# Expert stage of a four-layer network: 25 tiles of 256 slots and 21 of 128 in place of 39 tiles of 256

## The chip, the cores and the metric

The kernel runs on one core of a Trainium2 chip, as one program. The metric is the device time of one execution in microseconds (us). The core has five engines that run side by side: PE (TensorE, matrix products and transposes, results in PSUM), DVE (VectorE), ACT (ScalarE), POOL (GpSimd, here mostly the issuer of indirect DMAs) and SP (SyncE, which issues plain DMAs). Each engine works through its own instructions in order and waits on semaphores for the others. Loading a stationary operand into PE is shown as a row of its own, PEld.

## The reference

Four layers work on x, four images of 256 channels and 32 x 32 points, that is 4096 tokens of 256 values. Layer 0 is a state-space layer, layer 1 a non-local gate. Layer 2 is attention and then a mixture of experts; layer 3 is a form of attention without a score matrix and then an LSTM over 1024 steps. The change lies in the mixture of experts:

```python
# layer 2 (the lines that matter; t is (4, 1024, 256))
t = t + _L2_attn_ref(_ln_t(t), ...)
t = t + _L2_ffn_ref(_ln_t(t), Wg, bg, W1, b1, W2, b2)   # TOP_K = 2, E = 8, H = 1024
```

In `_L2_ffn_ref` a gate (Wg, bg) picks the two best of eight experts for each token and weighs them with a softmax over the two. Expert e computes gelu(u W1[e] + b1[e]) W2[e] + b2[e], with W1[e] 256 x 1024 and W2[e] 1024 x 256. A token's result is the weighted sum of its two experts. That makes 8192 pairs of token and expert, split over the experts as the gate decides: the counts are known only at run time. Everything is f32.

## The kernel before

Layer 2 is `_layer2`: `_layer2_attention` goes over the four images, and `_layer2_experts` then runs the experts. `_head` prepares one image for the experts: it normalises the tokens, computes the gate, gives each pair a slot in a DRAM array `sorted` (one region of 4096 rows for each expert) and scatters the normalised rows, with their weight and their place in the result, to these slots by indirect DMAs from POOL (16 for an image, L1005). The head of image b runs beside the attention of image b + 1. Heads are generators; `beside(n)` and `next(parts, None)` take a few of their instructions between others. The head of the last image runs beside the first expert tiles.

A tile is 256 slots of one expert (TS = 256), two blocks of 128 (A = 2). Since counts are unknown when the program is built, the number of tiles is the one that always suffices: NTILE = 2 * 4096 / 256 + 7 = 39. Each expert's last tile may be partly empty; its empty slots are sent to rows of `results` that nothing reads. NFULL = 16 tiles are certain to be full from the first three images alone: `_first_tiles` finds their experts and slots, so that they can start before the last image's head is done. `_other_tiles` finds those of the other 23. `_table`, `_pick` and `_weight_rows` are their helpers: small DVE operations on tables of tiles by experts.

`_layer2_experts` then does for each tile j:

1. `gathered(j)`: POOL fetches the expert's weights, one row of 4360 floats for each of 128 partitions (2.23 MB, L1193), into one of three buffers (`moe_w1` holds one, `moe_w` two, chosen by j % 3), and the 256 rows, one indirect DMA for each block of 128 (L1198), into one of three `row` buffers. DVE copies the rows' places to `place` (L1207, L1209; three buffers). PE transposes the rows (four transposes to `pt`, L1213) and DVE copies them to `uT` (L1215).
2. The first product (L1230): for each of eight blocks of 128 hidden units, W1 is stationary and uT's 256 slots are moving, twice (256 inputs = 2 x 128). ACT applies gelu with the bias (L1234) and writes `hT`. The hidden units lie on the partitions, as the second product wants them.
3. The second product (L1244): for each block of 128 slots, eight products with hT stationary and W2 (256 columns) moving. DVE adds the bias (L1251) and multiplies by the weight (L1252); POOL scatters the 128 rows to `results` (L1253).

In the source `gathered(j + 1)` stands in the middle of the second product of tile j. Tile pools and a scheduler settle the order of each engine's instructions: an instruction can be moved ahead of others that don't bind it. In the built program POOL's order is: the scatter of tile t's first block, the weights of tile t + 3 (their buffer is that of tile t; they wait for its last reader, the bias addition L1251), the scatter of the second block, the rows of tile t + 3. `place` of a tile stands on DVE just ahead of the `uT` of the tile before it. The indirect DMAs take eight semaphores in turn, so that each also waits for the eighth before it.

During eight tiles SP loads one eighth of the tokens back into `x` for layer 3 (`x<-tokens`, 512 KB each, L1261). Layer 3 begins when the last scatter has landed.

Of the kernel before, what the change touches and what calls it, by code (L numbers as in the profile page):

```python
# [44 lines left out]
NTILE = 2 * T // TS + E - 1  # L45
# [3 lines left out]
NFULL = (2 * (T - L) - E * (TS - 1)) // TS  # L49
# [30 lines left out]
def _setup(s):  # L80
# [55 lines left out]
    s.results = nc.dram_tensor("results", (2 * T + NTILE * TS, D), F32, kind="Internal").ap()  # L136
# [579 lines left out]
def _layer2(s):  # L716
# [4 lines left out]
    with ExitStack() as ctx:  # L721
# [6 lines left out]
            row=ctx.enter_context(tc.tile_pool(name="moe_row", bufs=3)),  # L728
            scatters=[], full=[],
# [21 lines left out]
        first = _layer2_attention(s, m)  # L751
        _layer2_experts(s, m, first)


def _layer2_attention(s, m):
    nc, tc = s.nc, s.tc
    scale = D**-0.5
    with ExitStack() as ctx:
# [14 lines left out]
        first = None  # L773
        for b in range(B):
# [80 lines left out]
            if b == B - 1:  # L855

                first = _first_tiles(s, m)
    return first
# [225 lines left out]
def _first_tiles(s, m):  # L1084
# [3 lines left out]
    over = m.one.tile([P, E, NCH], F32, name="f_over")  # L1088
    edges = m.one.tile([P, NCH], F32, name="f_edges")
    nc.vector.tensor_scalar(edges, m.marks[:, :NCH], float(TS), float(TS), ALU.mult, ALU.add)  # L1090
    nc.vector.tensor_tensor(over, _bc(m.counts, 2, NCH), _bc(edges, 1, E), ALU.is_ge)
    full = m.one.tile([P, E], F32, name="f_full")
    nc.vector.tensor_reduce(full, over, AX.X, ALU.add)
    expert, mine, first = _table(s, m, "f", NFULL, full)
    rows = _weight_rows(s, m, "f", expert)

    base = m.one.tile([P, E], F32, name="f_base")
    nc.vector.tensor_scalar(base, first, -float(TS), 1.0, ALU.mult, ALU.add)
    nc.vector.tensor_add(base, base, m.first)
    at = _pick(s, m, "f", mine, base)  # L1100
    nc.vector.scalar_tensor_tensor(
        at, m.marks[:, :NFULL], float(TS), at, ALU.mult, ALU.add
    )
    slots = m.keep.tile([P, NFULL, 2], U32, name="f_slots")
    nc.vector.tensor_tensor(slots, _bc(at, 2, 2), _bc(s.token[:, :2], 1, NFULL), ALU.add)

    taken = m.keep.tile([P, E], F32, name="f_taken")
    nc.vector.tensor_scalar(taken, first, -1.0, float(NFULL), ALU.mult, ALU.add)
    nc.vector.scalar_tensor_tensor(taken, taken, 0.0, full, ALU.max, ALU.min)
    return rows, slots, taken  # L1110


def _other_tiles(s, m, taken):
# [3 lines left out]
    n = NTILE - NFULL  # L1117
    over = m.one.tile([P, E, NCH], F32, name="o_over")
    edges = m.one.tile([P, NCH], F32, name="o_edges")
    nc.vector.tensor_scalar_mul(edges, m.marks[:, :NCH], float(TS))  # L1120
    nc.vector.tensor_tensor(over, _bc(m.counts, 2, NCH), _bc(edges, 1, E), ALU.is_gt)
    tiles = m.one.tile([P, E], F32, name="o_tiles")
    nc.vector.tensor_reduce(tiles, over, AX.X, ALU.add)
    nc.vector.tensor_sub(tiles, tiles, taken)
    yield
    expert, mine, first = _table(s, m, "o", n, tiles)
    rows = _weight_rows(s, m, "o", expert)
    yield

    base = m.one.tile([P, E], F32, name="o_base")  # L1130
    nc.vector.tensor_sub(base, taken, first)
    own = _pick(s, m, "o", mine, base)
    nc.vector.tensor_add(own, own, m.marks[:, :n])
    yield
    at = m.one.tile([P, n, 2], F32, name="o_at")
    nc.vector.scalar_tensor_tensor(
        at, _bc(own, 2, 2), float(TS), _bc(s.token[:, :2], 1, n), ALU.mult, ALU.add
    )
    held = _pick(s, m, "o_held", mine, m.counts)
    yield  # L1140
    valid = m.one.tile([P, n, 2], F32, name="o_valid")
    nc.vector.tensor_tensor(valid, at, _bc(held, 2, 2), ALU.is_lt)

    nc.vector.tensor_scalar_add(expert, expert, -float(E))
    nc.vector.scalar_tensor_tensor(
        at, _bc(expert, 2, 2), float(T), at, ALU.mult, ALU.add
    )
# [5 lines left out]
    slots = m.keep.tile([P, n, 2], U32, name="o_slots")  # L1153
    nc.vector.tensor_copy(slots, at)
    yield
    added = m.keep.tile([P, n, 2], F32, name="o_added")
    nc.vector.tensor_scalar(valid, valid, -1.0, 1.0, ALU.mult, ALU.add)
    ahead = m.one.tile([P, n, 2], F32, name="o_ahead")
    nc.gpsimd.iota(
# [8 lines left out]
def _layer2_experts(s, m, first):  # L1168
# [3 lines left out]
    with ExitStack() as body:  # L1172
# [15 lines left out]
        def gathered(j):  # L1188
# [8 lines left out]
            for a in range(A):  # L1197
# [4 lines left out]
                if j < NFULL:  # L1202

                    m.full.append(got)
# [675 lines left out]
```

## Time and profile before

| what | us |
|---|---|
| median of 3 runs (3463.36 to 3467.37) | 3466.0 |
| the profiled execution, its own time | 3467.84 |
| span of the profile | 3465.9 |
| first weight fetch to the end of the last expert tile | 764 to 1362 |
| one expert tile, undisturbed | 14.26 |
| PE busy over the span | 3237.8 (93%) |
| DVE, ACT, POOL busy over the span | 1998.7, 1253.7, 399.1 |

The page's row of 40 slices shows where the stage lies (each slice is 86.6 us; slices 9 to 16 are the experts):

```profile
PE   7788899989999997899999999999999999999888
PEld 4465354447888886578888888888888888888776
DVE  5696434452211112747777777777777777776666
ACT  4633222223222221433433434334343343433333
POOL 0182002222533331000000000000000000000000
```

A busy PE means that a product was under way, and the ends of products are modelled, so the time of a tile is read from the starts of its instructions in the timeline. A line of the timeline has start and length in us, engine, source line, operation, what it writes and reads, shapes and count, and in square brackets the idle time before it and what ended it. In the groups the last column is the idle time of the engine just before them.

### The profile page before, as it was taken

To read this page: it belongs to the slowest core of one execution; us is meant where nothing else is said; L and a number is where in the kernel's file an instruction comes from. 1 tells how busy PE (TensorE), PEld (TensorE's weight loads), DVE (VectorE), ACT (ScalarE), POOL (GpSimd) and SP (SyncE) were. 2 spreads that over 40 slices of the span, in tenths; PEclk is the share of its full clock that TensorE was granted. 3 is DMA by queue.
4 is the path that set the end of the run, shared out by engine and by line. 5 is a ranking of instruction groups with operands and counts; after the bars stand their busy time and mean duration, and the time that the engine had idled before them with its cause. 6 is when DMAs were issued, how large, how long until landed. Compare 5 with 4: busy or idle time off the path is not lost.

```text
span 3465.9 us, 147036 instructions
## 1 busy us (share of the span) xinstructions
PE 3237.8 (93%) x65492; PEld 2546.7 (73%) x65492; DVE 1998.7 (58%) x8361; ACT 1253.7 (36%) x5081; POOL 399.1 (12%) x490
## 2 busy tenths in 40 slices
PE   7788899989999997899999999999999999999888
PEld 4465354447888886578888888888888888888776
DVE  5696434452211112747777777777777777776666
ACT  4633222223222221433433434334343343433333
POOL 0182002222533331000000000000000000000000
PEclk9899899999999998899999999999999999999999
DMA  1290001124556554100000000000000000000000
GB/s 68 78 298 25 0 0 37 37 100 165 198 197 224 209 193 162 49 2 5 4 11 4 4 11 4 5 10 4 11 4 5 10 4 5 10 5 4 10 4 10
DMA packets 79355, 189.58 MB, mean 55 GB/s; under 512 B 6592, under 2 KB 64256, under 8 KB 73728
## 3 DMA queue, kind: packets, MB, share of 16 engines
q0 software_dynamic: 16176, 116.06, 9.1%
q1 hardware_dynamic: 60624, 59.12, 5.8%
q8 instruction: 512, 8.39, 1.0%
q10 hardware_dynamic: 1920, 5.00, 0.4%
q14 instruction: 123, 1.01, 0.1%
HBM read 119.14 MB, written 61.02 MB: 52 GB/s over the span
## 4 chain that ended last, share of the span: by engine, by line
PE 46%; DVE 9%; ACT 4%; issue 2%; DMA 0%; ACTq 0%; SPq 0%; DVEq 0%
PE p_c L1721 11%; PE p_c L1712 8%; DVE turned L1762 6%; PE p_i L1712 5%; PE p_i L1721 5%; PE p_o L1721 5%; PE p_o L1712 5%; PE beside L1662 4%; ACT a_o L1763 2%; DVE x L1775 2%; ACT th L1773 1%; PE beside L1569 1%; PE p_u L1441 1%; PE p_mm L1412 1%; PE beside L1602 1%
## 5 line engine op out<-in xcount | busy, mean ns | idle before, releaser
L1763 ACT ACTIVATE add<-turned 128x8 f32<-128x8 f32 x1024 | 214.3, 209 | 1011.3 <-DVE turned L1762 1011.3
L1721 PE MATMUL p_c<-w_v,x 128*4 128x64 f32 x16368 | 416.6, 219 | 61.6 <-DVE x L1775 58.4
L1712 PE MATMUL p_c<-xg,shift 128*128 128x64 f32 x2048 | 446.0, 299 | 0.0
L1721 PE MATMUL p_i<-w_v,x 128*4 128x64 f32 x16368 | 417.4, 219 | 0.0
L1721 PE MATMUL p_o<-w_v,x 128*4 128x64 f32 x16368 | 417.3, 219 | 0.0
L1712 PE MATMUL p_i<-xg,shift 128*128 128x64 f32 x2048 | 407.0, 280 | 0.0
L1762 DVE STREAM_TRANSPOSE turned<-p_c 128x64 f32<-128x64 f32 x1024 | 255.9, 250 | 252.7 <-PE p_c L1721 219.4
L1712 PE MATMUL p_o<-xg,shift 128*128 128x64 f32 x2048 | 396.4, 275 | 0.0
L1712 PEld LDWEIGHTS p_c<-xg,shift 128*128 128x128 f32 x2048 | 304.9, 188 | 117.6 <-DVE turned L1762 0.4
L1721 PEld LDWEIGHTS p_c<-w_v,x 128*4 128x4 f32 x16368 | 228.0, 85 | 183.8 <-DVE x L1775 102.9
L1775 DVE TENSOR_TENSOR x<-a_o,th 128x8 f32<-128x8 f32 x1024 | 171.8, 168 | 246.6 <-ACT th L1773 246.6
L1712 PEld LDWEIGHTS p_o<-xg,shift 128*128 128x128 f32 x2048 | 311.4, 192 | 0.0
L1712 PEld LDWEIGHTS p_i<-xg,shift 128*128 128x128 f32 x2048 | 305.1, 188 | 0.0
L1230 PE MATMUL ph<-uT,w 128*128 128x256 f32 x1248 | 284.9, 386 | 19.0 <-DVE uT L1215 19.0
L1234 ACT ACTIVATE hT<-ph,w 128x256 f32<-128x256 f32 x312 | 147.9, 474 | 391.7 <-PE ph L1230 391.6
L1721 PEld LDWEIGHTS p_i<-w_v,x 128*4 128x4 f32 x16368 | 281.8, 87 | 0.5
L1244 PE MATMUL po<-w,hT 128*128 128x256 f32 x1248 | 282.0, 379 | 0.0
L1721 PEld LDWEIGHTS p_o<-w_v,x 128*4 128x4 f32 x16368 | 281.9, 87 | 0.0
L1230 PEld LDWEIGHTS ph<-uT,w 128*128 128x128 f32 x1248 | 240.4, 194 | 56.0 <-DVE uT L1215 22.2
L1762 DVE STREAM_TRANSPOSE turned<-p_i 128x64 f32<-128x64 f32 x1024 | 271.6, 265 | 1.1 <-PE p_i L1721 0.5
L1244 PEld LDWEIGHTS po<-w,hT 128*128 128x128 f32 x1248 | 234.1, 190 | 30.2
L1762 DVE STREAM_TRANSPOSE turned<-p_o 128x64 f32<-128x64 f32 x1024 | 255.9, 250 | 0.4 <-PE p_o L1721 0.3
(447 smaller groups left out, 4400.2 us busy)
## 6 DMA issues: line engine op xcount, KB each, us to landing
sorted<-zeros SPq DMA_DIRECT2D x32, 1032.0 KB, 15.0
y_in<-results SPq DMA_DIRECT2D x16, 512.0 KB, 6.0
x<-in_x_dram SPq DMA_DIRECT2D x8, 512.0 KB, 8.7
tokens<-rows SPq DMA_DIRECT2D x4, 1024.0 KB, 4.4
x<-tokens SPq DMA_DIRECT2D x8, 512.0 KB, 4.2
out_dram<-x_l SPq DMA_DIRECT2D x64, 64.0 KB, 1.7
results<-y,place POOLq DMA_INDIRECT x78, 4.3
w_l<-in_w_l_dram ACTq DMA_DIRECT2D x1, 1092.0 KB, 11.4
```

What stands on the lines that cost most here:

```text
L1230: nc.tensor.matmul(ph, w1[:, k, bass.ts(n, P)], uT[:, k, :], start=k == 0, stop=k == C - 1,)
L1234: nc.scalar.activation(hT[:, n, :], ph, AF.Gelu, bias=b1[:, n : n + 1])
L1244: nc.tensor.matmul(po, hT[:, n, bass.ts(a, P)], w2[:, n, :], start=n == 0, stop=n == NHC - 1,)
L1412: nc.tensor.matmul(p, wk[:, k, bass.ts(m, P)], u[:, k, b * L + i * W : b * L + (i + 1) * W], start=k == 0, stop=k == C - 1,)
L1441: nc.tensor.matmul(pu[c], rows[:, n, bass.ts(c, P)], kt, start=n == 0, stop=n == TPI - 1,)
L1569: nc.tensor.matmul(p, lhs[:, k, b, bass.ts(m, P)], rhs, start=k == 0, stop=k == C - 1)
L1662: nc.tensor.matmul(p[bass.ts(i, R), :], rows[:, k, bass.ts(g, R)], w_u[:, k, at : at + GQ // GC], start=k == 0, stop=k == C - 1, tile_posi ...
L1712: nc.tensor.matmul(p[:, :H], shift[:, row * B : row * B + P], xg[n][:, g, bass.ts(i, H)], start=True, stop=t == 0,)
L1721: nc.tensor.matmul(p[R * i : R * i + B, :H], hs[:, t - 1, bass.ts(k, B)], w_v[:, k, i * GQ + g * H : i * GQ + (g + 1) * H], start=False, s ...
L1762: nc.vector.transpose(zt.rearrange("p c w -> p (c w)"), pz[g][:, :H])
L1763: nc.scalar.activation(dst.rearrange("p (c b) -> p c b", c=C), zt[:, :, :B], f)
L1775: nc.vector.tensor_mul(h, a_o, th)
```

## The change

The 39 tiles become NTILE = 46: 17 full tiles from the first three images ("first"; rounded up where it was rounded down), 8 more full tiles that are certain once all four images are counted ("more"), and 21 half tiles of 128 slots for the rest. The order is the 17 first, then each of the 8 with two or three halves behind it (2, 3, 2, 3, 3, 2, 3, 3).

`_first_tiles` becomes the generator `_full_tiles`, called twice, and `_other_tiles` becomes `_half_tiles`, with the same small operations on one block for each tile. `gathered` is split: `fetched(j)` issues the DMAs and is called two tiles ahead, `turned(j)` copies the places and transposes the rows, and is called one tile ahead, ahead of the second block's product in a full tile and after the first four transposes in a half. The `row` pool has four buffers in place of three. The tokens are loaded back after each full tile of the second kind.

A half tile's first product is turned: uT's 128 slots are stationary and W1 is moving, 512 columns at a time (two PSUM banks, twice each). The result has the slots on the partitions; DVE copies it to SBUF (`raw`), PE transposes it in eight blocks of 128, and ACT applies gelu to each block of 128 columns. The second product is as before, once.

```diff
-NTILE = 2 * T // TS + E - 1
...
-NFULL = (2 * (T - L) - E * (TS - 1)) // TS
+NFULL = -(-(2 * (T - L) - E * (TS - 1)) // TS)
+NMORE = -(-(2 * T - E * (TS - 1)) // TS) - NFULL
+NHALF = (2 * T + E * (P - 1)) // P - 2 * (NFULL + NMORE)
+NTILE = NFULL + NMORE + NHALF
...
-            row=ctx.enter_context(tc.tile_pool(name="moe_row", bufs=3)),
+            row=ctx.enter_context(tc.tile_pool(name="moe_row", bufs=4)),
...
+    order = [("first", i) for i in range(NFULL)]
+    for i in range(NMORE):
+        order.append(("more", i))
+        order += [("half", h) for h in range(i * NHALF // NMORE, (i + 1) * NHALF // NMORE)]
...
         def last_image():
             yield from _head(s, m, B - 1, psum)
-            yield from _other_tiles(s, m, taken)
-
-        def gathered(j):
...
+            yield from _full_tiles(s, m, "more", NMORE, m.tiles["first"][2])
+            yield from _half_tiles(s, m, m.tiles["more"][2])
+
+        parts = last_image()
+
+        def fetched(j):
+
+            kind, i = order[j]
+            if kind != "first":
+                for _ in parts:
+                    pass
+            rows, slots = m.tiles[kind][:2]
             w = (wp if j % 3 else m.w).tile([P, NEXP], F32, name="w")
             nc.gpsimd.indirect_dma_start(
                 w, None, s.d["w12"], bass.IndirectOffsetOnAxis(rows[:, i : i + 1], 0)
             )
-            row = m.row.tile([P, A, ROW], F32, name="row")
+            A = slots.shape[2]
+            row = m.row.tile([P, 2, ROW], F32, name="row")
             for a in range(A):
...
+            return w, row[:, :A]
+
+        def turned(j):
...
+            place = rp.tile([P, 2], U32, name="place")[:, :A]
+            if kind == "half":
+                nc.vector.tensor_add(place, row[:, :, D + 1], m.tiles[kind][2][:, i, :])
+            else:
                 nc.vector.tensor_copy(place, row[:, :, D + 1])
...
+        held = {j: fetched(j) for j in range(2)}
+        ahead = turned(0)
+        for j, (_, tile) in enumerate(order):
+            if j + 2 < NTILE:
+                held[j + 2] = fetched(j + 2)
...
+            else:
+
+                raw = rp.tile([P, HID], F32, name="raw", bufs=2)
+                for i in range(HID // W):
+                    ph = ps.tile([P, W], F32, name="ph")
+                    for k in range(C):
+                        nc.tensor.matmul(
+                            ph, uT[:, k, :], w1[:, k, bass.ts(i, W)],
+                            start=k == 0, stop=k == C - 1,
+                        )
+                    nc.vector.tensor_copy(raw[:, bass.ts(i, W)], ph)
+                for i in range(HID // W):
+                    ph = ps.tile([P, W], F32, name="ph")
+                    for n in range(TPB):
+                        nc.tensor.transpose(
+                            ph[:, bass.ts(n, P)], raw[:, bass.ts(i * TPB + n, P)], s.ident
+                        )
+                    for n in range(TPB):
+                        gelu(i * TPB + n, ph[:, bass.ts(n, P)])
+                    if i == 0 and j + 1 < NTILE:
+                        ahead = turned(j + 1)
             for a in range(A):
+                if a == A - 1 == 1 and j + 1 < NTILE:
+                    ahead = turned(j + 1)
                 po = ps2.tile([P, D], F32, name="po")
...
-                if a == 0 and j + 1 < NTILE:
-                    ahead = gathered(j + 1)
...
-            if NFULL <= j < NFULL + NBLK:
-
-                i = j - NFULL
+            if j >= NFULL and A == 2:
+
                 got = nc.sync.dma_start(
-                    s.xr[:, bass.ts(i, TPB), :],
-                    s.tokens[bass.ts(i, W), :].rearrange("(n p) c -> p n c", p=P),
+                    s.xr[:, bass.ts(tile, TPB), :],
+                    s.tokens[bass.ts(tile, W), :].rearrange("(n p) c -> p n c", p=P),
                 )
```

Built, the changed program has POOL in the same order as before for weights (tile t + 3 behind tile t's last bias addition, the second scatter behind it). The rows of a tile now stand one tile earlier. `place` stands two tiles ahead of its use: of tile t + 3 behind the second scaling of tile t where t is full, of tile t + 2 ahead of the `raw` copies of tile t + 1 where tiles t and t + 1 are halves. It still has three buffers, so it waits for the scatter that last read its buffer: the one of tile t in the first case, of tile t - 1 in the second. The first tile's instructions up to its `uT`, and all of layer 3, stand in the same order.

## The prediction

> **What bounds the kernel now.** I read the page's parts 1, 2 and 5, then busy time by stretch of time, then the timeline of one tile of the expert stage, then its waits. All edits lie in that stage, from 764 us (first weight fetch) to 1362 us; the recurrence behind it (over 2000 us) is the same program before and after.
>
> ```profile
> L1230 PE MATMUL ph<-uT,w 128*128 128x256 f32 x1248 | 284.9, 386 | 19.0 <-DVE uT L1215 19.0
> L1234 ACT ACTIVATE hT<-ph,w 128x256 f32<-128x256 f32 x312 | 147.9, 474 | 391.7 <-PE ph L1230 391.6
> ...
> L1244 PE MATMUL po<-w,hT 128*128 128x256 f32 x1248 | 282.0, 379 | 0.0
> ```
>
> 1248 records over 39 tiles: 32 for each product of a tile. ACT waits for PE (391.6), hardly ever the reverse.
>
> ```profile
> 764.00:781.50 17.50, 9.48 (x29) 4.25 (x27) 2.65 (x6) 0.00 (x0) 8.76 (x10) 0.88 0.92 362
> ...
> 880.00:920.00 40.00, 33.14 (x148) 28.49 (x147) 5.29 (x16) 8.53 (x18) 23.73 (x26) 0.92 0.54 188
> ...
> 1000.00:1362.20 362.20, 360.67 (x1716) 315.77 (x1714) 56.07 (x151) 94.83 (x200) 117.02 (x120) 1.00 0.52 189
> ```
>
> Columns: stretch, length, busy us of PE, weight load, DVE, ACT, POOL; clock, DMA share, GB/s. From 1000 us on PE is busy 360.67 of 362.20 us: PE is the bound, and the DMA engines are half idle. In 764 to 781.5, with three fetches back to back, they moved 362 GB/s.
>
> ```profile
> 1191.04 7.07 PE L1230 MATMUL ph<-uT,w 128*128 128x256 f32 x32
> ...
> 1191.24 0.42 DVE L1251 TENSOR_TENSOR y<-po,w 128x256 f32<-128x256 f32 x1 [1.95 <-PE po L1244]
> ...
> 1192.44 0.96 POOL L1193 DMA_INDIRECT w<-in_w_dram,o_rows  x1 [1.87 <-issue]
> ...
> 1197.95 3.62 PE L1244 MATMUL po<-w,hT 128*128 128x256 f32 x16
> ...
> 1201.40 0.60 PE L1213 MATMUL pt<-ident,row 128*128 128x128 f32 x4
> ...
> 1201.84 3.62 PE L1244 MATMUL po<-w,hT 128*128 128x256 f32 x16
> ...
> 1204.17 0.99 POOL L1253 DMA_INDIRECT results<-y,place  x1 [6.94 <-DVE y L1252]
> ...
> 1205.30 7.07 PE L1230 MATMUL ph<-uT,w 128*128 128x256 f32 x32
> ```
>
> One tile: 1205.30 - 1191.04 = 14.26 us without a gap: 6.91 first product, 3.45 + 0.44 + 3.46 for the rest.
>
> ```profile
> 903.36 0.17 DVE L1207 CAST place<-row 128x2 uint32<-128x2 f32 x1 [11.42 <-DMA row<-sorted,f_slots]
> ...
> 914.70 0.17 DVE L1207 CAST place<-row 128x2 uint32<-128x2 f32 x1 [9.47 <-DMA row<-sorted,f_slots]
> 914.77 0.69 DVE L1215 COPY uT<-pt 128x512 f32<-128x512 f32 x1
> ```
>
> The exception. The slot numbers ("place") of a later tile stand on DVE ahead of the next tile's uT. At 914.70 they waited for rows that POOL had issued late, behind 16 scatters of the last image; PE stood 6.86 us, and the product after it took 9.69 instead of 7.07 us at a lower clock: 9.5 us. A second stall, 4.78 us at 830, comes from DVE's wait for the store of tokens (9.49 us). Two small ones (1.5 us) follow after 1000 us.
>
> **What the Trainium skill says.** "TensorE: Matmul & The Clock Gate", Back-to-back issue gap: 262 cycles for 256 columns, 518 for 512. The trace agrees in proportion: a 256-column record every 0.216 us (16 in 3.45), a 512-column one every 0.43 (two at 705.82 take 1.02, less the 0.592 of the last). Each is twice the page's time, and an f32 product is two records. Same page, LDWEIGHTS: the load goes by the 128 stationary columns. The trace has 0.190 us in f32, which 0.216 just covers and the 0.108 of a 128-column product would not; hence the turned form. Same page, Architectural detail: VectorE is strict FIFO; the uT behind its place at 914.77 agrees. "DMA: Bandwidth & Descriptors", SWDGE vs HWDGE vs iDMA: only one SWDGE queue is allocated. It agrees: the result scatter at 1204.17, alone, landed after 2.4 us, the one issued 1.27 us behind a weight fetch after 8.3.
>
> **The change part by part.**
>
> *Tiles.* 39 of 256 slots become 25 of 256 and 21 of 128: 78 halves of work become 71. Old 39 x 14.26 = 556.1 us. A full tile costs 14.26; one followed by a half transposes two blocks fewer, 14.04 (0.11 per transpose: eight at L835 take 1.04, less the last's 0.272).
>
> *A half.* First product 8 records x 0.43 = 3.44; eight transposes 0.88; next tile's two 0.22; second product 16 x 0.216 = 3.46: 8.00 us. New on DVE: two copies 128x512 from PSUM, 0.684 each (row of L1215). The first ends at 2.6 and is covered. The second starts when the second block's last record ends (3.01 + 0.59 = 3.60), ends at 4.3; with 0.1 for the hand-over, PE could have gone on at 4.10 and waits until 4.45. So 8.35 us. Before a full tile two more transposes fill part of that wait; I leave 8.35. Were the copies fully hidden it is 8.0; with 0.5 us of weight load exposed, 8.85. Gelu on 128 columns isn't in the trace: 209 ns at 8 columns (L1763), 474 at 256, so by a straight line 337; eight are 2.7 us, at most 3.8. Beside 3.46 us of the second product, the first half of them already during the transposes: nothing. If each took 474, the last product would wait up to 0.5 us.
>
> 17 x 14.26 + 8 x 14.04 + 21 x 8.35 = 242.4 + 112.3 + 175.4 = 530.1: **-26.0 us**.
>
> *Fetches.* Seven more weight fetches of 2.23 MB. "Two ahead" alters little for them: in the program before, POOL already has the fetch for tile t+3 right after tile t's y (1192.44: tile t's y add ended at 1191.66), when its buffer is free; it is the same after. Needed two tiles later: 16.7 us over two halves, against landing times of 9.3 us (10.7 beside a token load): no wait for PE. Load: a half moves 2.49 MB, 6.9 us at 362 GB/s, under 8.35. POOL issues three DMAs per half, 3 x 1.27 = 3.8 us: hidden. Rows gain a fourth buffer and so arrive a tile earlier.
>
> *Place.* It is now in the order two tiles further ahead, behind tile t's second y. With three place buffers it waits until t's own scatter has landed: 1.39 us from a tile's end to the fetch, 1.27 to the scatter, 8.3 to land: 11.0 us after the tile's end. Behind it on DVE: the next tile's first y (10.4) and uT, due at 14.26. For full tiles that is covered (uT ends at 12.3, 2 us to spare). Between two halves the order differs: place waits for the scatter of the tile before, and behind it are the copies that PE needs. In 8 of 13 such passages that tile was a full one, whose token load (0.5 MB, by SP) runs beside the fetch: in the profile scatters then land after 9.3 to 10.9 us, median 9.8, so 12.5 after the tile's end, 4.1 into the second half. Copies end at 5.7, transposes begin 1.35 later than in 8.35: 8 x 1.35 = **+10.8**. At the other five the scatter (11.0) is in by 2.7: nothing. Bounds: 0 if the scatters land in 8.3, 30 if they take 2 us more at all 13 passages.
>
> *The stall at 915.* The place that caused it moves behind the tile; but place for tile 8 (counted from 0) now waits for a scatter issued at about 892 behind 13 of the last image, in at about 894.6: uT 1.7 us late; the next one's scatter follows a fetch at 902 and lands near 912: 3.1 us late. 9.5 becomes 4.8: **-4.7**; bounds -9.5 and +5. The two small stalls: **-1.5**. Start (the same order up to the first uT), the 830 stall, the tables (about 20 short DVE operations more, between other work) and the token loads (last one some 27 us before the end; they land in 4.2): nothing.
>
> Sum: -26.0 + 10.8 - 4.7 - 1.5 = -21.4. The profiled execution took 3467.84 (span 3465.9 and 1.9 around it): 3446.4. The runs' median, 3466.0, is 1.8 lower: **3445**.
>
> **Rivals.** (a) No place ever holds the copies, the stall at 915 goes: -26.0 - 9.5 - 1.5 = -37: **3429**. For it: 0.5 MB is a small load, and DMA is half idle. Against: the eight landing times. (b) Fetches of successive halves queue up, and each of 13 passages loses 1.5 us more: +19.5: **3464**, no change. For it: 6.9 of 8.35 us is tight. Against: 362 GB/s held over three fetches. (c) Slower: the weight fetch becomes the bound from the 17th tile on. 29 fetches; the stage may take 530.1 - 242.4 + 32 = 320 us until nothing is gained, so it decides from 11.0 us per fetch; at 11.5, 333 us: **3479**. For it: landings of 10.7 beside token loads. Against: that holds 2 us of latency, and fetches overlap. (d) That the change doesn't do what it says is part of the above: the weights are fetched no further ahead.
>
> **How the numbers follow.** Forecast 57%, (a) 20%, (b) 14%, (c) 9%. The forecast's own spread, from 8.0 to 8.6 us per half and half to one and a half times the two place terms, is 3436 to 3454. The range 3427 to 3460 adds (a) and a third of (b). 0.2% is 7 us, about what a measurement of this kernel can tell: faster (below 3459) is the forecast, (a) and a sixth of (b), 80%; same 11%; slower 9%.
>
> **What would show it.** A full tile at 14.26 and a half at 8.0 to 8.4 in the timeline; the second half after a full tile near 9.7, its idle time put down to DVE, and DVE's to place and the result scatter; PE idle near 890 to 915 below 6 us; weight landings at 9 to 11 us and no wait of the first product for w. It is wrong if halves stand apart by 9 us or more without place in front, if the first product waits for w, or if a uT of full tiles is late.

## The result, and the profile after

| | median us | lowest to highest, runs |
|---|---|---|
| before | 3463.36 | 3461.96 to 3467.37, 5 |
| changed | 3451.04 | 3447.67 to 3454.62, 5 |
| ratio | 0.9962 | 95% interval 0.9948 to 0.9977 |

The changed kernel is faster by 12 us; 3445 was predicted. Its profiled execution took 3454.62 us, with a span of 3452.9; the one of before took 3467.84, with a span of 3465.9. So the two profiles stand 13.2 us apart, where the prediction's sum was 21.4.

I cut the spans at the starts of the tiles' first products. Tiles are counted from 0; "start" runs from the start of the attention's last product to tile 0.

| stretch, us | before | changed | difference | predicted |
|---|---|---|---|---|
| start, and tiles 0 to 5 | 108.3 | 108.2 | -0.1 | 0 |
| tiles 6, 7, 8 | 52.4 | 60.9 | **+8.5** | -4.7 |
| tiles 9 to 16 | 114.0 | 114.0 | 0 | 0 |
| tile 17 to the last expert product | 316.1 | 299.2 | **-16.9** | -16.7 |
| on to layer 3's first product | 21.3 | 20.0 | -1.2 | 0 |
| layer 3 and the LSTM | 2082.2 | 2079.1 | -3.1 | 0 |

The -16.7 is -26.0 for the tiles, +10.8 for the held second halves and -1.5 for the two small stalls. The last row is the same program in both; over all profiles of this study it lies between 2076.3 and 2083.3 whatever the kernel, so a difference of 3 us in it means nothing. What the prediction missed is in the second row. All stretches below are read from one profile each.

The changed kernel's groups, shapes apart (records, then busy us, mean ns of one, and the engine's idle time just before them with what ended it):

```profile
L1299 PE MATMUL po<-w,hT 128*128 128x256 f32 x1136 | 259.5, 382 | 0.0
L1265 PE MATMUL ph<-uT,w 128*128 128x256 f32 x800 | 187.7, 392 | 21.3 <-DVE uT L1239 10.3 <-ACT hT L1257 8.0 <-issue 3.0
...
L1279 PE MATMUL ph<-w,uT 128*128 128x512 f32 x168 | 75.5, 592 | 0.0
...
L1257 ACT ACTIVATE hT<-ph,w 128x128 f32<-128x128 f32 x168 | 45.6, 382 | 176.9 <-issue 92.3 <-PE ph L1287 84.6
...
L1283 DVE COPY raw<-ph 128x512 f32<-128x512 f32 x42 | 28.2, 688 | 23.7 <-PE ph L1279 23.7
L1287 PE MATMUL ph<-ident,raw 128*128 128x128 f32 x168 | 26.4, 280 | 13.1 <-DVE raw L1283 12.0
```

The 25 full tiles show 800 records of the first product, the 21 halves 168 turned ones and 168 transposes. The second product has 1136 records where it had 1248: that is the work saved. The other side of the account is in the last columns: 21.3 us of PE's idle time before first products, 8.0 of it for ACT, which was not among the waits of that product before, and 12.0 us before the transposes of the halves.

The stretches that the prediction showed of before, the last 0.2 us shorter (length; PE, weight load, DVE, ACT and POOL; clock, DMA share, GB/s):

```profile
764.00:781.50 17.50, 9.26 (x27) 4.12 (x25) 2.35 (x6) 0.00 (x0) 10.96 (x12) 0.88 0.90 354
880.00:920.00 40.00, 29.03 (x105) 22.44 (x104) 5.10 (x21) 7.36 (x16) 20.55 (x22) 0.74 0.44 155
...
1000.00:1362.00 362.00, 340.76 (x1516) 264.84 (x1514) 82.26 (x202) 90.07 (x262) 111.95 (x115) 0.99 0.65 241
```

From 1000 us on the DMA engines moved 241 GB/s in place of 189, still well below the 354 of the first stretch. In 880 to 920 PE was busy for 29.03 us where it had been busy for 33.14: the loss there, which was to shrink, has grown.

Two halves behind a full tile, from the timeline (start, length, instruction; in brackets the idle time before it and what ended it):

```profile
1141.06 3.60 PE L1279 MATMUL ph<-w,uT 128*128 128x512 f32 x8
...
1144.70 0.69 DVE L1283 COPY raw<-ph 128x512 f32<-128x512 f32 x1 [1.02 <-PE ph L1279]
...
1145.44 0.65 PE L1287 MATMUL ph<-ident,raw 128*128 128x128 f32 x4
...
1149.39 3.60 PE L1279 MATMUL ph<-w,uT 128*128 128x512 f32 x8
...
1153.68 0.17 DVE L1233 CAST place<-row 128x2 uint32<-128x2 f32 x1 [3.27 <-DMA results<-y,place]
1153.76 1.28 DVE L1283 COPY raw<-ph 128x512 f32<-128x512 f32 x2
...
1154.50 0.65 PE L1287 MATMUL ph<-ident,raw 128*128 128x128 f32 x4 [1.51 <-DVE raw L1283]
...
1159.32 4.05 PE L1265 MATMUL ph<-uT,w 128*128 128x256 f32 x18
```

The first half takes 1149.39 - 1141.06 = 8.33 us. In the second, DVE comes to the slot numbers of a later tile, finds their buffer still held by a scatter under way, and stands 3.27 us. Both copies of `raw` are queued behind it, PE waits 1.51 us for them, and the half takes 9.93 us. This is the hold that was forecast, at the place where it was forecast. PE waits for little else after 1000 us; one line of the waits answers for it (us, times, longest):

```profile
PE ph L1287 <- DVE raw L1283: 12.0, 9, 1.8
```

What went wrong is the seventh tile, index 6:

```profile
879.64 2.75 PE L1265 MATMUL ph<-uT,w 128*128 128x256 f32 x12
884.08 0.47 ACT L1257 ACTIVATE hT<-ph,w 128x256 f32<-128x256 f32 x1 [11.11 <-remote]
...
884.61 1.13 PE L1265 MATMUL ph<-uT,w 128*128 128x256 f32 x4 [2.22 <-issue]
889.65 0.47 ACT L1257 ACTIVATE hT<-ph,w 128x256 f32<-128x256 f32 x1 [5.10 <-remote]
...
890.18 2.08 PE L1265 MATMUL ph<-uT,w 128*128 128x256 f32 x4 [4.44 <-ACT hT L1257]
```

A first product normally runs as one group of 32 records in 7.07 us. Here it comes in fours. The products at 879.64 should have given ACT its first gelu about 1.1 us later; it starts at 884.08, the next at 889.65, and "remote" means that the trace shows no instruction of the program that ended ACT's wait. PE then has no free PSUM tile and waits for ACT (those are the 8.0 us of the groups). The last gelu of the tile starts some 20 us after the first, against 6.0 in a tile of 14.25 us, and the tile takes 32.42 us in place of 14.25. The stall at 915 that the prediction describes is not in this profile: tiles 7 and 8 take 14.25 us each. No step of the prediction had the slow tile.

### The profile page after: what moved, and what is told of

It is laid out like the page before. It is cut to its first block, busy times and chain, and to the rows that moved or that the text cites. A ratio compares the mean times of both kernels' runs of the same rounds, so it can differ in the third digit from the quotient of the medians.

```text
span 3452.9 us, 146712 instructions
## 1 busy us (share of the span) xinstructions
PE 3212.0 (93%) x65254; PEld 2489.5 (72%) x65254; DVE 2024.1 (59%) x8425; ACT 1242.7 (36%) x5137; POOL 392.2 (11%) x483
## 4 chain that ended last, share of the span: by engine, by line
PE 46%; DVE 9%; ACT 4%; issue 2%; DMA 0%; ACTq 0%; SPq 0%; DVEq 0%
PE p_c L1772 11%; PE p_c L1763 8%; DVE turned L1813 6%; PE p_i L1763 5%; PE p_o L1772 5%; PE p_i L1772 5%; PE p_o L1763 5%; PE beside L1713 4%; ACT a_o L1814 2%; DVE x L1826 2%; ACT th L1824 1%; PE beside L1620 1%; PE p_u L1492 1%; PE p_mm L1463 1%; PE beside L1653 1%
## 5 line engine op out<-in xcount | busy, mean ns | idle before, releaser
L1257 ACT ACTIVATE hT<-ph,w 128x256 f32<-128x256 f32 (+1 forms) x368 | 140.0, 432 | 397.5 <-PE ph L1265 167.9
L1299 PE MATMUL po<-w,hT 128*128 128x256 f32 x1136 | 259.5, 382 | 0.0
L1814 ACT ACTIVATE a_o<-turned 128x8 f32<-128x8 f32 x1024 | 213.4, 208 | 94.8 <-DVE cell L1817 3.6
L1739 POOL TENSOR_TENSOR x_l<-x_l,x 128x128 f32<-128x128 f32 x56 | 26.9, 517 | 1827.4 <-DVE x L1826 1419.4
L1299 PEld LDWEIGHTS po<-w,hT 128*128 128x128 f32 x1136 | 213.8, 191 | 28.1
```

What stands on the lines that cost most here:

```text
L1257: nc.scalar.activation(hT[:, n, : A * P], ph, AF.Gelu, bias=b1[:, n : n + 1])
L1299: nc.tensor.matmul(po, hT[:, n, bass.ts(a, P)], w2[:, n, :], start=n == 0, stop=n == NHC - 1,)
L1814: nc.scalar.activation(dst.rearrange("p (c b) -> p c b", c=C), zt[:, :, :B], f)
```

## The experiments

Three questions were open. On the slow seventh tile: is it made by the change (by its order of DMAs), or does it come with the execution, so that it would hit the kernel before as well? On the held halves: do the slot numbers alone hold them, or fetches too? And one reason of the prediction, that a 128-column product would be bound by its weight load, had not been measured at all.

**The changed kernel again** (no edit).

> The changed kernel once more, for the 32.4 us that the seventh tile (first product at 879.6) took in its profile in place of 14.3: the first product's blocks went out late one after another, ACT waiting for them, while no wait of the program explains it. Theory S1: an accident of that one execution; here the seventh tile takes 14 to 15 us, and the eighth or ninth shows the stall that the prediction has there, 4 to 10 us; the stage then ends some 5 to 13 us earlier than at 1353.7. Theory S2: it belongs to the program; again 25 us or more between the starts of the seventh and eighth tile. In both the passages from a first half after a full tile to the next stay at 8.33 us and from the second half at 9.3 to 10.1, and the median is 3447 to 3455.

Measured 3453.29 (3451.16 to 3461.03), ratio 0.9965 (0.9951 to 0.9978). The slow tile came again: 29.48 us in the profile. Held second halves: 12.6 us in all, 11.9 in the first profile. So the stall wasn't a single accident; whether it was the change's was open.

**Slot numbers computed behind their own tile's first bias addition**, instead of a tile or two ahead:

```diff
-            place = rp.tile([P, 2], U32, name="place")[:, :A]
...
-            return place, uT
+            return uT
...
-                nc.vector.tensor_add(y, po, b2)
+                added = nc.vector.tensor_add(y, po, b2)
+                if a == 0:
+                    place = rp.tile([P, 2], U32, name="place")[:, :A]
+                    put = ...            # the same copy or addition
+                    tc.add_manual_dep(put.ins, added.ins.name, ...)
```

> The slot numbers of a tile are copied behind its own first bias addition, not two tiles ahead, so that they never stand ahead of the copies of a half and find their buffer free. Theory P1: the wait of the slot numbers for a scatter is what holds the second half of each group: all halves then stand 8.33 us apart, the eight waits of 0.8 to 1.8 us (11.9 us in sum) go, and the median is 10 to 14 us below the changed kernel's, near 3439. Theory P2 (rival): the copies would have waited anyway, for rows or for scatters that hold y; the second halves stay at 9.3 us or more and the gain is under 4 us. For the stall near 880 to 915 both expect no more than a few us of difference.

Measured 3432.44 (3428.48 to 3438.28), ratio 0.9898 (0.9883 to 0.9914). The same two halves in its timeline:

```profile
1140.62 3.60 PE L1274 MATMUL ph<-w,uT 128*128 128x512 f32 x8
...
1141.28 0.16 DVE L1303 TENSOR_TENSOR place<-row,h_added 128x1 uint32<-128x1 f32 x1
...
1142.54 0.69 DVE L1278 COPY raw<-ph 128x512 f32<-128x512 f32 x1 [0.83 <-PE ph L1274]
...
1148.95 3.40 PE L1260 MATMUL ph<-uT,w 128*128 128x256 f32 x15
```

The slot numbers wait for nothing now, and the second half takes 1148.95 - 1140.62 = 8.33 us. All halves do: the last stretch of the table went from 300.0 (the profile of the repeat) to 287.4. So the hold is the whole difference between a second half and another. The change of order gave 20.9 us by the medians, more than the hold: tile 0's `uT` had been behind slot numbers too. PE waited 5.86 us for it in the changed kernel and 0.40 here, of which about 1.6 us were left by the start of tile 1, since tile 0 itself took 21.25 us. (In the three later profiles that have late slot numbers and no slow seventh tile, tile 0 took 14.8 to 16.2 us; there the start and tiles 0 to 5 took 100.8 to 101.5 us, some 7 us less than the 108.6 of the changed kernel without a slow tile.) The rest is a slow seventh tile that was 2.7 us shorter in this profile (three tiles 55.3 against 58.0) and the noise of layer 3 (2076.3 against 2081.2).

**Halves as full tiles are done**: W1 stationary and 128 slots moving, no `raw`, no second set of transposes; slot numbers as in the change.

```diff
-            if A == 2:
-                for n in range(NHC):
-                    ph = ps.tile([P, W], F32, name="ph")[:, :TS]
...
-            else:
-                raw = rp.tile([P, HID], F32, name="raw", bufs=2)
...
+            for n in range(NHC):
+                ph = ps.tile([P, W], F32, name="ph")[:, : A * P]
+                for k in range(C):
+                    nc.tensor.matmul(ph, w1[:, k, bass.ts(n, P)], uT[:, k, :], ...)
+                gelu(n, ph)
...
+                if A == 1 and n == 3 and j + 1 < NTILE:
+                    ahead = turned(j + 1)
```

> Halves with W1 stationary and 128 slots moving, as a full tile does it, without the copies and the transposes back. Theory T1 (the prediction's reason for the turned form): each of the 32 records is bound by its weight load of 0.19 us, so the first product takes 6.1 us, a half 6.1 + 0.22 + 3.46 = 9.8 us and the 21 halves cost 21 x 1.45 = 30 us more, less the 11.9 of the held copies, which do not exist here: 15 to 22 us above the changed kernel, near 3469. Theory T2: a record of 128 columns takes 0.11 us with loads hidden; a half takes 7.2 us and the kernel is 20 us or more faster than the changed one.

Measured 3427.45 (3424.87 to 3430.72), ratio 0.9881 (0.9866 to 0.9896). From its timeline (PEld is the weight load):

```profile
1115.21 0.55 PE L1237 MATMUL pt<-ident,row 128*128 128x128 f32 x3 [2.39 <-DMA row<-sorted,more_slots]
...
1135.22 1.95 PE L1264 MATMUL ph<-uT,w 128*128 128x128 f32 x16
...
1137.11 1.86 PEld L1264 LDWEIGHTS ph<-uT,w 128*128 128x128 f32 x16
1137.22 1.95 PE L1264 MATMUL ph<-uT,w 128*128 128x128 f32 x16
...
1142.46 1.95 PE L1264 MATMUL ph<-uT,w 128*128 128x128 f32 x16
```

Sixteen loads in 1.86 us, sixteen products with their starts 0.112 us apart: the loads hide. A half takes 1142.46 - 1135.22 = 7.24 us, against 8.33 for the turned form. The theory that the load binds is wrong. What is left shows in the first line: at the last half before a full tile, PE waits for the rows of the full tile. Four such halves took 11.76, 13.66, 8.66 and 8.75 us; the other three, with the same transposes, took 7.46, so 13.0 us are lost there. 7.4 us of them are PE's waits for rows; most of the rest are slower products after the two longest waits, 2.39 and 2.99 us. (In the 6.2 us after each, the granted clock was 0.72 and 0.50, and PE lost another 1.8 and 3.1 us; after the other two waits, of about 1 us, it lost nothing.)

**Three `row` buffers in the changed kernel** (`bufs=4` to `bufs=3` of `moe_row`).

> The row buffers back from four to three, all else as changed; rows are then fetched a tile later, as before the change. Theory R1: the fourth buffer only lets the slot numbers move ahead; with three they stand one tile later and wait for rows in place of a scatter. Full tiles stay at 14.25 us, the held second halves change by less than 1 us each, the median moves by less than 8 us. Theory R2: rows late by one tile hold the transposes of halves; halves of 9 us and more throughout, 15 us or more above the changed kernel.

Measured 3447.48 (3445.34 to 3451.61), ratio 0.994 (0.9924 to 0.9955). The fourth buffer is worth nothing here: the hold summed to 10.3 us, and the seventh tile took 29.42. With three buffers the slot numbers of the held halves wait for rows, 1.9 to 2.7 us, where they had waited for a scatter.

**The kernel before again** (no edit).

> The kernel before once more, for its profile beside those of the changed ones. In these the seventh tile takes 27 to 32 us: the completions of its first product come 2 to 5 us apart while the last image's 16 scatters go out, and the time is not put down to any engine. Theory S2a: this belongs to the changed programs; here the seventh and eighth tile take 14.25 us each and the ninth begins after the stall shown before (6.9 us idle, about 9.5 in all). Theory S2b: the first profile of the kernel before missed it, and it comes and goes with any program; here too a tile near 880 takes over 25 us.

One run, 3462.38. Its timeline around the seventh tile:

```profile
874.68 2.75 PE L1230 MATMUL ph<-uT,w 128*128 128x256 f32 x12
...
883.53 1.13 PE L1230 MATMUL ph<-uT,w 128*128 128x256 f32 x4 [1.69 <-issue]
887.23 0.47 ACT L1234 ACTIVATE hT<-ph,w 128x256 f32<-128x256 f32 x1 [3.75 <-remote]
887.76 2.08 PE L1230 MATMUL ph<-uT,w 128*128 128x256 f32 x4 [3.10 <-issue]
...
897.09 0.47 ACT L1234 ACTIVATE hT<-ph,w 128x256 f32<-128x256 f32 x1 [3.03 <-remote]
902.05 7.07 PE L1230 MATMUL ph<-uT,w 128*128 128x256 f32 x32
```

The same pattern: products in fours, gelus 1.4 to 4.2 us apart, two of them after a wait that nothing in the trace ended, the tile 902.05 - 874.68 = 27.37 us. So the slow seventh tile isn't made by the change. And in this profile too the stall at 915 is missing where the slow tile comes: both next tiles take 14.25. The first profile of before, from which the prediction was made, had happened to be one without it.

**Late slot numbers and plain halves together.**

> Halves with W1 stationary (as e3) and the slot numbers behind the tile's own first bias addition (as e2). In e3 a half took 7.25 us, but 14.4 us were lost on the passages from the last half of a group to the next full tile, where the transposes waited for rows. Theory Q1: those rows are late because the slot numbers hold DVE and with it the bias additions that free the weight buffers; without the hold the fetches go out earlier, the passages shrink to 7.3 to 7.5 and the median is 8 to 15 us under e3, 3412 to 3420. Theory Q2: at 7.25 us a half the fetches (2.5 MB, 6.9 us at the 362 GB/s of the start) are the bound; the waits for rows stay and the gain is under 4 us.

Measured 3423.68 (3420.4 to 3426.06), ratio 0.9872 (0.9856 to 0.9889): the gain over plain halves alone is 3.8 us by the medians, as if the two edits hardly added. In the profile the stretch from tile 17 did shrink, 278.9 to 272.7, and the four last halves to 9.46, 9.11, 9.14 and 8.99 us. Neither theory holds as it stands: the median's gain is the small one of Q2, the passages shrank, but not to Q1's 7.5. PE's four waits for rows fell only from 7.4 to 6.0 us; as none is longer than 1.78 now, no slower products follow them, and that is most of the 6.1 us. What is left there is the wait for rows.

**The last image's scatters spread over tiles**, on the changed kernel: two beside each tile, each tied to the newest scaling of `y`, since the last late gelu of the slow tile (903.70 us in the changed kernel) started soon after the last of these scatters was issued (899.58).

```diff
             if b == B - 1:
                 m.scatters.append(done)
+                s.tc.add_manual_dep(done.ins, m.latest.ins.name, ...)
...
+        if b == B - 1:
+            for _ in range(8):
+                yield
...
-                done = nc.vector.tensor_scalar_mul(y, y, row[:, a, D : D + 1])
+                m.latest = done = nc.vector.tensor_scalar_mul(y, y, row[:, a, D : D + 1])
```

> The changed kernel with the last image's 16 scatters let out two beside each tile, from the seventh on, in place of one after another within 27 us. Theory B1: it is this dense row of scatters that holds the completions of the seventh tile's products; without it the seventh, eighth and ninth tile take 14.25 us each (42.8 us against 57 to 61), the median is 12 to 18 us under the changed kernel's 3451 to 3453, near 3437. Theory B2: each scatter costs PE its share wherever it stands; eight tiles then take 1.5 to 2 us more each and the time is within 4 us of the changed kernel's. The held second halves (9.3 to 10.1 us) stay in both.

Measured 3448.37 (3446.33 to 3453.89), ratio 0.9955 (0.994 to 0.997). The seventh tile took 14.25 us, but later tiles lost about 1 us each: tiles 6 to 16 together 165.5 us, against 163.9 in the profile of the changed kernel without a slow tile (below). That would point to the scatters as the cause, but the next kernel, measured in the same session with the scatters as they were, had no slow tile either. Nothing follows on the cause.

**The next tile's transposes behind the whole first product of a half** (`n == 3` to `n == NHC - 1`), on the kernel with late slot numbers and plain halves.

> e6 with the next tile's transposes behind the whole first product of a half, not in its middle. In e6 the last half of four groups took 9.0 to 9.5 us, the transposes waiting for rows of the next full tile. Theory Q3: those rows are 1.8 to 2.3 us late only for the place where they are read; 1.8 us later they are nearly in, the four passages take 7.3 to 7.8, 6 to 8 us are gained on e6 (3416). Theory Q2 again: the fetches are the bound and the wait moves elsewhere; under 3 us.

Measured 3406.93 (3399.11 to 3409.44), ratio 0.9826 (0.9806 to 0.9846). The stretch from tile 17 grew, 272.7 to 277.1, and the last halves took 12.01, 11.40, 8.61 and 9.09 us:

```profile
1093.06 0.55 PE L1232 MATMUL pt<-ident,row 128*128 128x128 f32 x3 [2.64 <-DMA row<-sorted,more_slots]
...
1093.44 5.31 PE L1274 MATMUL po<-w,hT 128*128 128x256 f32 x16
...
1098.59 7.07 PE L1259 MATMUL ph<-uT,w 128*128 128x256 f32 x32
```

PE came to the transposes later and still waited 2.64 us for the second block of rows; and the second product behind it took 5.31 us instead of 3.62: in 1093 to 1099 the granted clock was 0.72. The four waits sum to 7.0 us against 6.0; the rest of the 4.4 us lost is this slower product and another like it after a wait of 2.03 us. The edit did harm. The kernel is faster mainly because its profiled execution had no slow seventh tile (tiles 6 to 8: 42.76 against 55.6), and its tile 0 took 16.18 us against 20.45. It also shows late slot numbers without a slow tile for the first time: tiles 6 to 8 lose nothing at all, so the stall at 915 has gone with the hold.

**All four edits** (late slot numbers, plain halves, later transposes, spread scatters).

> All four together: plain halves, slot numbers behind the first bias addition, transposes behind the first product, scatters two beside each tile. With B1 and Q3 the gains add: e8 less 11 to 15 us, 3401 to 3407, 1.7 to 1.9% under the kernel before. With B2 it is within 4 us of e8.

Measured 3403.98 (3399.87 to 3404.96), ratio 0.9822 (0.9806 to 0.9838). From the attention's last product to the end of the experts it took 535.8 us, against 535.4 without the spreading: where no slow tile comes, spreading adds nothing.

**The changed kernel and the kernel before in one session, a third time** (no edits).

> The changed kernel a third time, beside the kernel before (e12) on the same chip in the same hour. So far the slow seventh tile (25 to 32 us) stood in seven profiles out of seven of two calls, of the changed kernels and of the kernel before alike, and in none of the four others. Theory C1: it comes with the execution's circumstances, not with the kernel; both profiles of this call show it or neither does. Without it the seventh to ninth tiles take 42.8 to 48 us (the late slot numbers of the prediction) and the median is 3436 to 3445; with it 57 to 61 and 3447 to 3455. Theory C2: it belongs to the changed kernel's own program; here it is again, whatever e12 shows.

> The kernel before, for its profile beside e10. C1: a seventh tile over 25 us here if e10 has one, else the stall of the first profile (9.5 us) or none. C2: no slow seventh tile.

The changed kernel 3446.35 (3445.14 to 3451.57, 6 runs), ratio 0.9943 (0.9928 to 0.9959). Measured beside it, the kernel before had a median of 3467.32 (3461.58 to 3477.48, 11 runs), so the change gained 21.0 us; its profiled execution took 3467.05. Neither profile has a slow seventh tile: the stall before is the one that the prediction describes, and the one after is what it became. Before, timeline of PE:

```profile
893.28 7.07 PE L1230 MATMUL ph<-uT,w 128*128 128x256 f32 x32
...
915.60 9.30 PE L1230 MATMUL ph<-uT,w 128*128 128x256 f32 x32 [7.90 <-DVE uT L1215]
```

After, timeline of all engines:

```profile
895.18 0.17 DVE L1233 CAST place<-row 128x2 uint32<-128x2 f32 x1 [11.36 <-DMA results<-y,place]
...
896.33 7.17 PE L1265 MATMUL ph<-uT,w 128*128 128x256 f32 x32 [1.40 <-DVE uT L1239]
...
913.37 0.17 DVE L1233 CAST place<-row 128x2 uint32<-128x2 f32 x1 [16.11 <-DMA results<-y,place]
...
914.55 8.66 PE L1265 MATMUL ph<-uT,w 128*128 128x256 f32 x32 [3.70 <-DVE uT L1239]
```

One wait of 7.90 us has become a small one of 1.40 and one of 3.70 at the tile after. Both long waits are followed by a slower first product, 9.30 and 8.66 us in place of 7.07, at a granted clock of 0.87 (916 to 931) and 0.91 (914.5 to 931). Tiles 6 to 8 took 53.05 us before and 49.87 after.

**Rows fetched ahead of weights** (in `fetched` the weight DMA behind the row DMAs), with late slot numbers, plain halves, spread scatters, and the transposes back in the middle of a half.

> As e9, with the next tile's transposes back in the middle of a half's first product and each tile's rows fetched ahead of its weights. Theory Q4: in e6 and e9 the last half of a group waited for rows that stood behind a weight fetch in the queue; ahead of it they are in time, these passages fall from 9 to 12 us to 7.3 to 7.8, from the eighteenth tile to the end 262 to 268 us (277.6 in e9), median near 3390. Theory Q2: the weight fetches themselves are the bound at 7.25 us a half; the wait moves to the first product and 272 us or more remain, 3397 to 3404.

Measured 3400.01 (3395.37 to 3401.07), ratio 0.98 (0.9783 to 0.9818), the fastest version of this study. The last half before a full tile, in PE's timeline:

```profile
1087.05 1.95 PE L1267 MATMUL ph<-uT,w 128*128 128x128 f32 x16
1088.83 0.60 PE L1240 MATMUL pt<-ident,row 128*128 128x128 f32 x4
1089.27 1.95 PE L1267 MATMUL ph<-uT,w 128*128 128x128 f32 x16
...
1094.51 7.07 PE L1267 MATMUL ph<-uT,w 128*128 128x256 f32 x32
```

No wait, 1094.51 - 1087.05 = 7.46 us (two transposes more than the other halves), at all of them; the stretch from tile 17 is 265.9 us. The fair comparison is late slot numbers with plain halves, where the transposes stand at the same place: 272.7, with last halves of 9.0 to 9.5. So the stretch agrees with Q4, though the median does not reach its 3390: between the profiles of all four edits and of this one the experts' part shrank by 12.3 us, but the part ahead of it grew by 5 us and layer 3 by 3. What the order did can be read from POOL's issues. With all four edits the second block of a full tile's rows, 0.13 MB, was issued behind a weight fetch that itself waited for its buffer; now it goes out some 5.5 us earlier, and from issue to landing it takes 7.9 to 8.1 us in place of 8.4 to 10.2 at these passages. So most of the gain is POOL's own order. The smaller part fits the Trainium skill's "DMA: Bandwidth & Descriptors", section SWDGE vs HWDGE vs iDMA, by which only one SWDGE queue is allocated: the rows no longer stand in it behind 2.2 MB more of weights.

## Why the prediction was right, and where not

*The sum.* In the pair of one session without a slow tile, the profiled executions took 3467.05 and 3445.31: -21.7 us, where -21.4 was predicted. By terms of the stretches: tile 17 to the end -15.1 (predicted -16.7), tiles 6 to 8 -3.2 (predicted -4.7), the end of the experts to layer 3 -0.9, layer 3 -3.8 (noise), everything ahead of tile 6 +1.5 (1.0 of it ahead of the experts). That it agrees to 0.3 us is luck: it owes some of its closeness to layer 3, without which the terms give -17.9, and single executions differ by several us. The medians of that session gave -21.0, those of the first session, with the slow tile in the changed kernel's profile, -12.3.

*The tiles, -26.0.* Right. A full tile before a half took 14.03 us (14.04 predicted), a half 8.33 (8.35); PE's wait for the second `raw` copy was the term that made 8.35 of 8.0, and it is there. Gelu on 128 columns took 382 ns by the groups (337 by the straight line) and was hidden, as argued.

*The hold, +10.8.* Mechanism and places right: of the 13 halves that follow a half, exactly the eight that come second behind a full tile are held; the other five take 8.33 (one of them 8.48 in the third profile). The forecast size was a little low: 1.49 us each in the first profile, 11.9 in all, and 12.6 and 14.2 in the repeats. Moving the slot numbers away removed it whole, so it is shown that they hold the halves. Why the scatter they wait for is late was not tested. The prediction put it down to the token load beside it, and its landing times fit: in the third profile the scatters issued just after a full tile, beside that load, landed after 9.8 to 11.0 us (forecast 9.8), the one after a full tile without such a load after 7.8, and those after a half after 7.1 to 10.5, median 8.6. But no run moves or leaves out the token load.

*The fetches, 0.* Right for PE: among its waits after 1000 us there is none for weights. Rivals (b) and (c), queueing fetches and a bound by weight fetches, are out for the kernel as changed; even with 7.24 us for a half and rows fetched first, PE's waits show none for weights.

*The stall at 915, 9.5 to 4.8.* This is the step that failed in the first session, though its picture of the waits was right: it said slot numbers at 894.6 and about 912, and 1.7 and 3.1 us late. In the changed kernel's profile without a slow tile they came at 895.18 and 913.37, and the three tiles took 1.56, 3.97 and 1.59 us more than 14.25: 7.1 in all. The third is the slower first product after the wait of 3.70 us; the prediction counted such a product in the 9.5 of before and left it out of its 4.8. Before, the same three tiles lost 9.7 and 10.3 in the two profiles without a slow tile. The term's size should have been about -3 rather than -4.7. What made +8.5 of it between the first two profiles was something that one profile of before couldn't show: a slow seventh tile in one execution and not in the other. With it in both, tiles 6 to 8 take 55.9 us before and 58.0 to 60.9 after, so the change gains nothing there and loses 2 to 5.

*The start, 0.* Right that nothing changed. But the slot numbers already held tile 0's `uT` in the kernel before (5.87 us of PE's waiting), and the prediction took that as given.

*The reason for the turned form.* Wrong, though no term of the sum hung on it: every cost of a half was worked out for the turned form, which was built. The prediction took a load record of 0.190 us and concluded that it "just covers" beside 0.216 and would not beside 0.108. The length of a record is not the spacing at which records can follow each other. The Trainium skill's "TensorE: Matmul & The Clock Gate", section Back-to-back issue gap, says that the spacing is set by product and load together, pipelined. The profile of before had an example on view: beside the four transposes at 1201.40, which the prediction shows, stand four loads,

```profile
1201.19 0.57 PEld L1213 LDWEIGHTS pt<-ident,row 128*128 128x128 f32 x4
```

and the transposes, on 128 columns, start 0.11 us apart. Measured in plain halves: 0.112 us, and 7.24 us for a half instead of 8.33.

*Rival (a)*, no hold and no stall at 915, is refuted for the kernel as changed, but late slot numbers make both true: the hold is gone in all profiles that have them, the stall in the three of them without a slow tile. That their own median, 3432.44, lies near the rival's 3429 is luck: in that profile a slow seventh tile still costs 12.6 us.

## What to carry to other kernels

A small copy that waits for a buffer holds everything queued behind it on its engine: put it behind the work that waits for nothing, next to its use, and the wait vanishes without another buffer. Where one engine issues large and small fetches in order, issue the small ones first if they are needed first: a large one that waits for its buffer holds them back. Test a reason like "the load would bind" by the spacing of starts in the trace, never by the length of one record. Take a second profile of the kernel before predicting from a stall: one execution may have another stall, or lack the one that the next has.

## What the runs showed of the hardware that was not expected

The slow seventh tile came in 7 of 14 profiles, among them one of the kernel before, and in none of the other seven. Of the four later sessions it came in every profile of two (four and two of them) and in none of the other two (three each). It isn't the chip alone: the second and the third of these sessions ran on the same one, and the slow tile came in the second only.

When it comes, the eight gelus of the tile take 16 to 20 us from the first start to the last against 6.0. Most start 1.4 to 5.6 us apart, and nearly all of these distances lie close to a multiple of 0.70 us (1.4, 2.1, 2.8, 3.5, 4.2, 4.9, 5.6); in three profiles the last two or three follow at once. These traces also lack 28 to 41 of PE's some 4,650 completion signals, the other seven none. But next to none is missing within the slow tile: 13 to 18 are missing ahead of it, nearly all after 600 us, and 11 to 27 behind it, where tiles take their usual time.

The granted clock in 880 to 920 is recorded as 0.74 in the changed kernel and 0.83 in its repeat. It can't explain the tile alone: by an estimate, 7.07 us of products would take 9.6 at 0.74. The Trainium skill's "TensorE: Matmul & The Clock Gate", section Seeing it yourself, warns that clock events in the trace are unreliable and that a clock has been seen stuck at a quarter for over 50 us. No run shows that here, and the twelve products at 879.64 speak against it: they start 0.216 us apart, the usual pace (12 in 2.75 us), while the gelu behind them comes 3.3 us late.

The slow tile ends within a few us of the issue of the last image's last scatter: its last late gelu starts from 3.2 us ahead of that issue to 4.1 behind it over the seven profiles. Spreading these scatters was tried only in sessions in which nothing had the slow tile. Whether the recording of the profile itself has a part was not tested either. Its cause stays open. Against three tiles of 14.25 us it costs 13 us in the kernel before and 15 to 18 in the changed one; but it stands in the place of the stall at 915, which costs 9.7 to 10.3 and 7.1, so that it adds about 3 us before and 8 to 11 after.

Waits of PE can cost more than their own length. From tile 6 on, outside the slow tile, the 14 profiles have ten waits of 2.0 us or more ahead of expert products (2.03 to 7.90). Behind nine of them the next products are slower and lose another 1.6 to 3.1 us in sum, at a recorded clock of 0.50 to 0.91 where it was read; behind one (2.57 us) nothing is lost. Of the waits of 0.9 to 1.9 us only one is followed by such a loss (1.77 us, with 2.0 lost).

A product on 128 columns with a fresh 128-column load for each costs hardly more per column than one on 256: a record every 0.112 us against one every 0.216.
